# Channels dealt three to a partition, and two turns moved from TensorE to VectorE

## The chip, the cores and the metric

The kernel runs on one core of one Trainium2 chip. The metric is the device time of a launch in microseconds (us); the times here are the median of three runs. A profiled execution is a further run of its own: its trace has a span, from the first to the last instruction, and the run a time of its own beside it.

On a core there are five engines with queues of their own: TensorE (PE in the profile, with its weight loads as PEld), VectorE (DVE), ScalarE (ACT), GpSimd (POOL) and SyncE (SP, which in this kernel only issues transfers). Sixteen DMA engines move data between DRAM and the on-chip memory SBUF. TensorE writes into PSUM, which is divided into banks.

## The reference

x has the shape (8, 56, 56, 384), float32: 8 images of 56 by 56 positions with 384 channels. Two layers follow one another, each of them `x = x + f(gn(x))`.

```python
def _gn(v, G=32, eps=1e-5):
    g = v.reshape(B_, H_, W_, G, C_ // G)          # 32 groups of 12 channels
    m = jnp.mean(g, axis=(1, 2, 4), keepdims=True)
    s = jnp.var(g, axis=(1, 2, 4), keepdims=True)
    return ((g - m) / jnp.sqrt(s + eps)).reshape(v.shape)

# layer 0: 12 heads of 32 channels, 9 by 9 weights at each position
v = einsum('bhwc,oc->bhwo', x, Wv)
a = einsum('bhwc,oc->bhwo', x, Wa)                 # 972 logits a position
attn = softmax(a * 32 ** -0.5)                     # over the 9 inputs q
out = einsum('bnhpq,bnqhd->bnphd', attn, v_unf)    # v_unf: the 3 by 3 neighbours of v
canvas[:, i:i + h, j:j + w] += out[:, :, :, p]     # each of 9 outputs added at its place
y = canvas[:, 1:-1, 1:-1];  return einsum('bhwc,oc->bhwo', y, Wo)

# layer 1: 6 heads of 64 channels, 9 weights at each position
a = softmax(x @ W_attn + b_attn);  v = x @ W_v + b_v
y = einsum('bpKhd,bphK->bphd', patches_of_v, a);  return y @ W_proj + b_proj
```

## The kernel before

**Tiling.** The 8 images are taken as 4 pairs (`NPAIR`). A pair has 56 columns, and a column of a pair is 112 rows (`R`: two images of 56). A projection contracts over channels, so most of the work is done with the channels on the partitions: a tile is [128 partitions, 3 chunks (`NCH`), columns, 112 rows], and chunk i holds the channels 128i to 128i+127. In DRAM the channels are innermost. x is therefore turned once on its way in and the result once on its way out.

**Layer 0** goes one column a step, 56 steps a pair and three more at the end. In a step:

- `attend` (L604) makes three products of 288 logits (`wa_t`) and one of 384 (`wv_t`), each from three chunks, into PSUM `bank`s. VectorE takes the maximum and the difference out of the bank, ScalarE the exponential, and ScalarE copies v out. Between the products the hook `between` puts in other work.
- A step later the weights are normalised (VectorE, then GpSimd); then terms of neighbouring columns are added (`presum`) and a matmul into `pw` adds those of neighbouring rows (`fold`). SP stores the results in a table in DRAM (`ztab<-wts`), GpSimd stores v in another (`vtab<-v`).
- Of eight columns (`SB`) one has no tile of its own: its 112 rows ride in the 16 unused rows of each of the seven others; `share_out` (L647) brings their weights together (`last<-at`, `at<-last` on SP; `at<-at` on GpSimd).
- Every 7 columns make a patch. SP loads its two halves of v (`vp<-vtab`) and of the folded weights (`z<-ztab`), TensorE contracts them (`pc<-z,vp`), ScalarE copies to `yT`, and six `project_out` (L833) multiply by `wo_t` into `po`, PSUM tag "o", one buffer. VectorE adds the residual (`x1t`) and takes its statistics, and SP stores `x1t` to DRAM as layer 1's input. `plan` (L791) gives each of these pieces the step at which it is due; two or three pieces run in a step.

While pair p is worked on, x of pair p+1 is turned, in 14 blocks of 4 columns (`XB`), three steps a block. `stats_load` (L432) is one transfer on SP's queue of 112 partitions by 1536 floats (`xr<-in_x`). `stats_chunk` (L443) runs once a step: four TensorE transposes into `pt` (PSUM tag "t"), a ScalarE copy to `xt`, and two `bn_stats` on VectorE. After three chunks `keep_block` stores the block in DRAM (`xT<-xt` on SP), from where it is loaded again as `xin` and `xres`. x of pair 0 is turned at the start, before the first step, in the same way through the large banks.

After the last block, `norm_params` (L268) puts together the statistics: six `bn_aggr`, then an average over each group for the mean and another for the variance (L274 `over_groups`), into `pgmean` and `pgvar`. A group of 12 channels can lie across two chunks, so an average is seven matmuls with the matrices `gmat` (built at L153 to L169 from a selector, through three matmuls at the start). `normed` (L575) applies scale and bias on ScalarE, one instruction for each chunk and image, two blocks ahead of the products.

**Layer 1** (L998) works in 32 patches of 7 columns: `attend` makes one product of 438 columns (54 logits and v) into one of two banks, GpSimd stores both (`at<-lgt`, `vtab<-v`; L1075 and L331), then `weigh`, `share`, `move` and `fetch` lead to contractions (`pc`) and six `project_out` (L1180), PSUM tags "o" and "f". `turn` (L1190) brings a column back: three TensorE transposes, a ScalarE copy to `ot`, and after each half patch (4 and 3 columns) one GpSimd transfer of 112 partitions by 1536 or 1152 floats. Columns 3 to 6 of a patch wait in the list `turning` and alternate with the next patch's contractions, which run two (`NC`) at a time.

**What sets the order.** Each engine runs its instructions in the order of the program (`keep_in_program_order`, `InOrder`). Pieces in `jobs` run once their step is due, as many as the step calls for. Transfers go through one queue for each issuing engine; SP's carries all of layer 0's loads and stores but those of v and `at<-at`.

Of the kernel before, what the change touches and what calls it, by code (L numbers as in the profile page):

```python
# [15 lines left out]
def two_outlook_layers(  # L16
# [81 lines left out]

    xf = x.rearrange("b y x c -> (b y) x c")
# [52 lines left out]
    near = [range(max(0, i - 1), min(NCH, i + 2)) for i in range(NCH)]  # L152
    gmat = [const.tile([P, len(near[i]), P], F32, name=f"gmat_{i}") for i in range(NCH)]  # L153
    with tc.tile_pool(name="ps_setup", bufs=2, space=PS) as ps_setup:
        gsel = yT_flat[:G, :C]
        gpsimd.memset(gsel, 1.0)
        gpsimd.affine_select(
            out=gsel, in_=gsel, compare_op=ALU.is_ge, fill=0.0,
            base=0, pattern=[[1, C]], channel_multiplier=-GC,
        )  # L160
        gpsimd.affine_select(
            out=gsel, in_=gsel, compare_op=ALU.is_ge, fill=0.0,
            base=GC - 1, pattern=[[-1, C]], channel_multiplier=GC,
        )
        for i in range(NCH):
            pg = ps_setup.tile([P, C], F32, tag="pg", name=f"pg_{i}")
            matmul(pg, gsel[:, i * P : (i + 1) * P], gsel, start=True, stop=True)
            lo, hi = near[i][0] * P, (near[i][-1] + 1) * P
            nc.vector.tensor_scalar_mul(gmat[i].rearrange("p j c -> p (j c)"), pg[:, lo:hi], 1.0 / GC)  # L169
# [93 lines left out]
    def weight(pool, src, n, name, queue=nc.sync):  # L263
        t = pool.tile([P, NCH, n], F32, name=name)
        queue.dma_start(t, src.rearrange("(i p) n -> p i n", p=P))
        return t

    def norm_params(st, name, params, key):  # L268

        mv = stat.tile([P, NCH, IMG, 2], F32, tag="mv", name=f"mv_{name}")  # L270

        def over_groups(src, what):
            pg = ps.tile([P, NCH, IMG], F32, tag="t", name=f"p{what}_{name}")
            for j in range(NCH):  # L274
                for i in near[j]:
                    matmul(
                        pg[:, j, :], gmat[i][:, j - near[i][0], :], src[:, i, :],
                        start=(i == near[j][0]), stop=(i == near[j][-1]),
                    )
            g = stat.tile([P, NCH, IMG], F32, tag=what, name=f"{what}_{name}")  # L280
            vector.tensor_copy(g, pg)
            return g

        for i in range(NCH):
            for b in range(IMG):
                vector.bn_aggr(mv[:, i, b, :], st[:, i, b, :, :])
        yield
        mean = over_groups(mv[:, :, :, 0], "gmean")

        part = stat.tile([P, NCH, IMG], F32, tag="part", name=f"part_{name}")  # L290
        vector.tensor_sub(part, mv[:, :, :, 0], mean)
        vector.tensor_mul(part, part, part)
        vector.tensor_add(part, part, mv[:, :, :, 1])
        yield
        var = over_groups(part, "gvar")
        std = stat.tile([P, NCH, IMG], F32, tag="std", name=f"std_{name}")
        scalar.activation(std, var, AF.Sqrt, bias=eps_t)
        scale = const.tile([P, NCH, IMG], F32, name=f"scale_{name}")
        vector.reciprocal(scale, std)
        bias = const.tile([P, NCH, IMG], F32, name=f"bias_{name}")  # L300
# [93 lines left out]
    scalar.dma_start(bo_t, bo1.rearrange("(i p) -> p i", p=P))  # L394
# [25 lines left out]
    def layer0(late, pools):  # L420
# [11 lines left out]
        def stats_load(pair, blk, queue, xr):  # L432
            queue.dma_start(xr, xf[pair * R : (pair + 1) * R, blk * XB : (blk + 1) * XB, :])
            xrs[pair, blk] = xr

        def xr_tile(pair, blk):
            return io.tile([P, XB, C], F32, tag="xr", name=f"xr_{pair}_{blk}")[:R]
# [5 lines left out]
        def stats_chunk(pair, blk, i):  # L443

            if blk == 0 and i == 0:
                stats[pair] = stat.tile([P, NCH, IMG, NBLK, 6], F32, tag="st0", name=f"st0_{pair}")
# [3 lines left out]
            if pair == 0:  # L450
                pt = bank(P, 0, XB * R).rearrange("p (m r) -> p m r", m=XB)
            else:
                pt = ps.tile([P, XB, R], F32, tag="t", name=f"pt_{pair}_{blk}_{i}")
            for j in range(XB):
                transpose(pt[:, j, :], xr[:, j, i * P : (i + 1) * P], ident[:R, :R])
            scalar.copy(xt[:, i], pt)
            yield
            for b in range(IMG):
                vector.bn_stats(stats[pair][:, i, b, blk, :], xt[:, i, :, b * H : (b + 1) * H])
# [54 lines left out]
        for blk in range(NBLK):  # L514
# [5 lines left out]
            if blk == 1:  # L520
                wv_t = weight(fixed, wv0, C, "wv0_t", sync)
# [31 lines left out]
        scalar.dma_start(wn, wa0.rearrange("(i p) n -> p i n", p=P))  # L553
# [21 lines left out]
        def normed(g, chunks, whole=True, shared=True, both=False):  # L575
# [3 lines left out]
            for i in chunks:  # L579
                for b in range(IMG):  # L580
                    rows = slice(b * H, (b + 1) * H)

                    def put(dst, src):
                        if both and b:
                            vector.tensor_scalar(
                                dst, src, scale[:, i, b : b + 1], bias[:, i, b : b + 1],
# [291 lines left out]
        def upkeep(step):  # L878
# [18 lines left out]
            if j < NCH and g < NPAIR * NBLK:  # L897
                normed(g, (j,))
# [406 lines left out]
```

## Time and profile before

| | before |
|---|---|
| runs: median (lowest to highest) | 3314.91 us (3310.96 to 3317.94) |
| the profiled execution | 3315.84 us |
| its span in the trace | 3314.0 us, mean granted TensorE clock 0.978 |
| a pair in layer 0, from the trace | 522.7 us: 56 steps of 9.33 us |
| a patch in layer 1, from the trace | 34.3 us |
| DMA moved in the span | 850.99 MB, mean 257 GB/s |

How to read it: the busy share of an engine is its working time over the span. The page gives it as a total and, in 40 slices of the span, in tenths. A line of a group names the source line, the engine, the operation, output and inputs with their shapes, how often it ran, then its total busy time in us, the mean of one in ns, and the idle time just before such instructions with what ended it. Layer 0 takes about the first 2200 us and layer 1 the rest.

### The profile page before, as it was taken

The page shows a single profiled execution, that of the slowest core. Times are in us where ns is not written, and L with a number is a line of the kernel's source. Part 1 is how long each engine was busy: PE and PEld are TensorE (multiplying, and loading weights), DVE is VectorE, ACT ScalarE, POOL GpSimd, SP SyncE. Part 2 cuts the span into 40 slices and gives each one's busy share as a digit, 9 for nine tenths or more (in the row PEclk, how much of TensorE's full clock was granted, in tenths as well). Part 3 has the DMA queues.
Part 4 walks back from the last instruction along what each step waited for, and adds up shares of the span by engine and source line. Part 5 has one row for each costly group of instructions (what it writes and reads, how often), then busy time and mean ns, then how long its engine had stood idle before and what let it go on. Part 6 is the DMA issues. An engine that isn't in the chain of part 4 may idle for free. (4 is left out here: it accounts for less than half of the span.)

```text
span 3314.0 us, 75237 instructions
## 1 busy us (share of the span) xinstructions
PE 3183.7 (96%) x28510; PEld 2186.6 (66%) x28510; DVE 1870.4 (56%) x4786; ACT 1366.3 (41%) x3749; POOL 1565.1 (47%) x2375
## 2 busy tenths in 40 slices
PE   7899999999999999999999999899999999999998
PEld 5567767776777667677666667556666666666665
DVE  5667776767777776777666677443333333333332
ACT  4444444444444444444343444234343443434432
POOL 2655555545555554455554555454343443434431
PEclk8899999999999999999999999899999999999999
DMA  9699988979897898899787888877778777787775
GB/s 294 201 308 295 303 274 270 292 258 304 300 315 235 279 308 266 290 294 300 229 257 259 288 253 294 285 240 212 220 215 233 212 216 226 220 222 214 223 215 155
DMA packets 554908, 850.99 MB, mean 257 GB/s; under 512 B 162174, under 2 KB 429954, under 8 KB 550450
## 3 DMA queue, kind: packets, MB, share of 16 engines
q1 hardware_dynamic: 448674, 672.76, 65.0%
q0 software_dynamic: 72016, 155.44, 14.7%
q10 hardware_dynamic: 33856, 17.98, 2.1%
q8 instruction: 225, 3.69, 0.5%
q14 instruction: 137, 1.12, 0.1%
HBM read 514.86 MB, written 322.17 MB: 253 GB/s over the span
## 5 line engine op out<-in xcount | busy, mean ns | idle before, releaser
L118 PE MATMUL bank<-wa_t,xn 128*128 128x288 f32 x3528 | 979.0, 415 | 3.5 <-ACT xn L133 2.1
L133 POOL TENSOR_TENSOR at<-at,den 128x972 f32<-128x972 f32 x196 | 440.5, 2247 | 859.3 <-DVE den L133 522.4
L118 PE MATMUL po<-yT,wo_t 128*128 128x448 f32 (+1 forms) x2304 | 821.0, 496 | 14.5 <-DVE x1t L133 12.0
L118 PEld LDWEIGHTS bank<-wa_t,xn 128*128 128x128 f32 x3528 | 652.9, 192 | 218.3 <-issue 22.2
L118 PEld LDWEIGHTS po<-yT,wo_t 128*128 128x128 f32 x2304 | 426.8, 191 | 296.0 <-issue 186.2
L133 ACT ACTIVATE at<-at 128x972 f32<-128x972 f32 (+1 forms) x228 | 215.8, 946 | 867.9 <-DVE at L133 860.5
L1075 POOL DMA_DIRECT2D at<-lgt x392 | 205.4, 527 | 616.3 <-DVE lgt L133 589.5
L118 PE MATMUL bank<-wc_t,xn 128*128 128x438 f32 x1176 | 477.8, 542 | 0.0
L133 DVE TENSOR_REDUCE mx<-bank 128x36 f32<-128x324 f32 x588 | 285.3, 485 | 340.6 <-PE bank L118 338.5
L118 PE MATMUL bank<-wv_t,xn 128*128 128x384 f32 x1176 | 417.3, 491 | 0.0
L118 PE MATMUL pc<-z,vp 121*32 121x49 f32 (+1 forms) x17664 | 374.7, 218 | 16.5 <-issue 10.3
L118 PEld LDWEIGHTS pc<-z,vp 121*32 121x32 f32 (+1 forms) x17664 | 337.8, 120 | 76.4 <-issue 51.0
L133 DVE TENSOR_TENSOR at<-bank,mx 128x324 f32<-128x324 f32 x588 | 291.4, 496 | 107.6 <-POOL pre L133 44.7
L118 PEld LDWEIGHTS bank<-wc_t,xn 128*128 128x128 f32 x1176 | 212.9, 190 | 169.4 <-issue 160.4
L118 PEld LDWEIGHTS bank<-wv_t,xn 128*128 128x128 f32 x1176 | 223.6, 192 | 134.8 <-issue 12.0
L133 DVE TENSOR_TENSOR lgt<-bank,ba_t 128x54 f32<-128x54 f32 x196 | 42.2, 215 | 455.8 <-PE bank L118 451.2
L133 POOL DMA_DIRECT2D vtab<-v x476 | 290.4, 614 | 14.4 <-issue 8.1
L133 ACT COPY yT<-pc 128x294 f32<-128x294 f32 (+2 forms) x512 | 195.7, 407 | 187.3 <-PE pc L118 186.4
L133 POOL TENSOR_TENSOR pre<-at,at 112x108 f32<-112x108 f32 (+1 forms) x440 | 224.4, 527 | 68.7 <-DMA at<-at 48.8
L133 DVE SCALAR_TENSOR_TENSOR x1t<-po,bo_t,x1t 128x448 f32<-128x448 f32 (+1 forms) x156 | 97.6, 626 | 249.5 <-PE po L118 249.5
L133 ACT COPY ot<-pt 112x384 f32<-112x384 f32 x128 | 61.2, 478 | 411.3 <-PE pt L121 411.0
L331 POOL DMA_DIRECT2D vtab<-v x392 | 211.4, 543 | 11.6 <-DMA vtab<-v 6.4
(118 smaller groups left out, 3279.0 us busy)
## 6 DMA issues: line engine op xcount, KB each, us to landing
z<-ztab SPq DMA_DIRECT2D x64, 2352.0 KB
vp<-vtab SPq DMA_DIRECT2D x64, 1536.0 KB
vp<-vtab SPq DMA_DIRECT2D x64, 945.0 KB
xres<-xT SPq DMA_DIRECT2D x32, 1176.0 KB
ztab<-wts SPq DMA_DIRECT2D x336, 110.2 KB
vtab<-v POOLq DMA_DIRECT2D x108, 336.0 KB, 6.2
xin<-xT SPq DMA_DIRECT2D x52, 672.0 KB
xr<-in_x SPq DMA_DIRECT2D x50, 672.0 KB
```

The lines of the kernel that those rows point to most:

```text
L118: tc.keep_in_program_order(nc.tensor.matmul(*args, **kwargs))
L133: return lambda *args, **kwargs: tc.keep_in_program_order(op(*args, **kwargs))
L331: queue.dma_start(bass.AP(table.tensor, table.offset + first, [*([line * step, count] for step, count in rows_of or ((1, rows),)), *([[(R ...
L1075: nc.gpsimd.dma_start(at_of(g_of)[row : row + n, m_of].rearrange("r k h -> r (k h)"), lg[lo : lo + n])
```

## The change

**The channels are dealt out.** Partition p of chunk i holds channel 3p+i, where it held 128i+p. The weights are loaded in that order (`rows_of_channels`), with three rows together on a partition. The output columns of the two output projections have to be in the same order, so that layer 0's result has its channels as x has; `wo0` and `wo1` are loaded as before into spare tiles and their columns sorted by three copies each (`sort_columns`: VectorE at steps 5 to 7, GpSimd at the start of layer 1).

**x of pairs 1 to 3 is turned by VectorE.** Four SP transfers bring a block, one for each set of 32 partitions, in the order of `by_quadrant`: 4 columns by 112 rows, each a piece of 96 floats. On a partition then lie 14 pieces of 96 floats, and one `vector.transpose` a chunk turns every third float of them, in 32 by 32 pieces, into `xt`. PSUM and ScalarE are not used for it. Pair 0's x is still turned by TensorE, with a stride of three.

**The results are turned by VectorE** straight after the residual is added, three turns a half patch, into `ot`, and leave in four GpSimd transfers a half. `turn` and `turning` go away, and contractions stand alone in their jobs. `project_out` alternates between the PSUM tags "o" and "t" in both layers, and layer 1's `attend` uses all three banks.

**One matmul an average.** 12 channels now lie on 4 whole partitions, so statistics are put together over the chunks by `bn_aggr` and one 128 by 128 matrix (1/4 where two partitions share a group) averages a group. Scale and bias are [128, 2], and `normed` does all chunks of an image in one instruction.

```diff
+    def by_quadrant(ap, r0, col, n, b):
+        first = r0 * W * C + col * C + b * QC
+        return bass.AP(ap.tensor, ap.offset + first, [[C, n], [W * C, R], [1, QC]])
...
+    gmat = const.tile([P, G, NPG], F32, name="gmat")
+    gpsimd.memset(gmat, 1.0 / NPG)
...
+    def rows_of_channels(t, src, queue):
+        queue.dma_start(t, src.rearrange("(p i) n -> p i n", i=NCH))
+
+    def sort_columns(t, by, i, engine):
+        engine(
+            t[:, i].rearrange("k (j p) -> k j p", j=NCH), by[:, i].rearrange("k (p j) -> k j p", j=NCH)
+        )
...
-            pg = ps.tile([P, NCH, IMG], F32, tag="t", name=f"p{what}_{name}")
-            for j in range(NCH):
-                for i in near[j]:
-                    matmul(
-                        pg[:, j, :], gmat[i][:, j - near[i][0], :], src[:, i, :],
-                        start=(i == near[j][0]), stop=(i == near[j][-1]),
-                    )
+            pg = ps.tile([P, IMG], F32, tag="t", name=f"p{what}_{name}")
+            matmul(pg, gmat, src, start=True, stop=True)
...
         def stats_load(pair, blk, queue, xr):
-            queue.dma_start(xr, xf[pair * R : (pair + 1) * R, blk * XB : (blk + 1) * XB, :])
             xrs[pair, blk] = xr
+            if not pair:
+                queue.dma_start(xr, xf[:R, blk * XB : (blk + 1) * XB, :])
+                return
+            for b in range(NQ):
+                queue.dma_start(
+                    xr[b * Q : (b + 1) * Q].rearrange("p a c -> p (a c)"),
+                    by_quadrant(x, pair * R, blk * XB, XB, b),
+                )
...
             else:
-                pt = ps.tile([P, XB, R], F32, tag="t", name=f"pt_{pair}_{blk}_{i}")
-            for j in range(XB):
-                transpose(pt[:, j, :], xr[:, j, i * P : (i + 1) * P], ident[:R, :R])
-            scalar.copy(xt[:, i], pt)
+                vector.transpose(
+                    xt[:, i].rearrange("p m r -> p (m r)").rearrange("p (k a) -> p a k", a=NB),
+                    xr[:, :, i::NCH],
+                )
...
+                    by = z_flat[0][:, : NCH * C].rearrange("p (i n) -> p i n", i=NCH)
+                    sync.dma_start(by, wo0.rearrange("(i p) n -> p i n", p=P))
+                if 5 <= c < 5 + NCH:
+                    by = z_flat[0][:, : NCH * C].rearrange("p (i n) -> p i n", i=NCH)
+                    sort_columns(wo_t, by, c - 5, vector.tensor_copy)
...
-            pa = bank(P, 0, NC1, 2)
+            pa = bank(P, 0, NC1)
...
-                po = ps.tile([P, 4 * R], F32, tag="of"[(half * NCH + j) % 2], name=f"po1_{g}_{half}_{j}")
+                po = ps.tile([P, 4 * R], F32, tag="ot"[(half + j) % 2], name=f"po1_{g}_{half}_{j}")
...
+                if j == 0:
+                    fetch.ot = io.tile([P, NB, QC], F32, tag="ot", name=f"ot_{g}_{half}")
+                vector.transpose(
+                    fetch.ot[:, :, j::NCH],
+                    x1t[:, j, hi - XB : hi].rearrange("p m r -> p (m r)").rearrange("p (k a) -> p a k", a=NB),
+                )
+                if j == NCH - 1:
+                    n = (hi - lo) * Q // XB
+                    for b in range(NQ):
+                        nc.gpsimd.dma_start(
+                            by_quadrant(out, pair * R, px * PX + lo, hi - lo, b),
+                            fetch.ot[(b + 1) * Q - n : (b + 1) * Q].rearrange("p a c -> p (a c)"),
+                        )
...
```

## The prediction

> **What bounds the kernel now.** I read the page first, then stretches of 100 us, then TensorE's timeline, then the groups with their shapes kept apart, and last the transfers.
>
> ```profile
> span 3314.0 us, 75237 instructions
> ...
> PE 3183.7 (96%) x28510; PEld 2186.6 (66%) x28510; DVE 1870.4 (56%) x4786; ACT 1366.3 (41%) x3749; POOL 1565.1 (47%) x2375
> ...
> DMA  9699988979897898899787888877778777787775
> ```
>
> TensorE is busy 96% of the span, so its work is what counts while nothing else fills up. Next is the DMA row: eights and nines for the first two thirds (layer 0), sevens after that (layer 1). Two stretches tell the layers apart (PE, PEld, DVE, ACT, POOL busy us, clock, DMA share, GB/s):
>
> ```profile
> 1400.00:1500.00 100.00, 99.69 (x866) 71.59 (x865) 75.72 (x203) 43.30 (x114) 48.73 (x65) 1.00 0.93 305
> 2700.00:2800.00 100.00, 100.00 (x795) 63.33 (x794) 31.88 (x69) 42.19 (x123) 41.80 (x80) 1.00 0.77 218
> ```
>
> Layer 1 is TensorE without a gap, everything else half free. In layer 0 TensorE is nearly as full, but the DMA engines stand at 0.93 and VectorE at 76%. What a turned block costs TensorE is read from the starts in its timeline: from a group's start to the next start.
>
> ```profile
> 806.81 1.62 PE L118 MATMUL bank<-wa_t,xn 128*128 128x288 f32 x6
> 808.26 0.55 PE L121 MATMUL pt<-ident,xr 112*128 112x112 f32 x4
> 808.65 2.43 PE L118 MATMUL po<-yT,wo_t 128*128 128x448 f32 x6
> ...
> 2702.04 0.49 PE L121 MATMUL pt<-ident,x1t 128*112 128x128 f32 x3
> 2702.36 1.86 PE L118 MATMUL po<-yT,wo_t 128*128 128x336 f32 x6
> ```
>
> Four transposes of x take 808.65 - 808.26 = 0.39 us and three of a result 0.32, less than their busy times of 0.55 and 0.49, because matmuls overlap. The groups that price the rest (busy us, mean ns of one, idle before):
>
> ```profile
> L121 PE MATMUL pt<-ident,xr 112*128 112x112 f32 x504 | 69.7, 260 | 7.4 <-DMA xr<-in_x 7.4
> L118 PE MATMUL pgvar<-part,gmat 128*128 128x2 f32 x112 | 20.3, 311 | 5.4 <-DVE part L133 4.5 <-DVE part L293 0.9
> L133 DVE TENSOR_TENSOR d<-at 128x432 f32<-128x432 f32 x196 | 118.7, 606 | 19.7 <-ACT at L133 19.5
> L133 DVE TENSOR_REDUCE mx<-at 112x42 f32<-112x378 f32 x32 | 26.7, 836 | 0.0
> L1048 POOL DMA_DIRECT2D wc_t<-in_wv x1 | 0.8, 767 | 0.0
> ```
>
> And the transfers that share SP's queue with the x loads:
>
> ```profile
> q1 hardware_dynamic: 448674, 672.76, 65.0%
> ...
> z<-ztab SPq DMA_DIRECT2D x64, 2352.0 KB
> ...
> xr<-in_x SPq DMA_DIRECT2D x50, 672.0 KB
> ...
> last<-at SPq DMA_DIRECT2D x140, 60.8 KB
> ```
>
> **What the change takes off TensorE.** Summed from start to next start over the whole timeline: the 504 transposes of x 54.4 us, the 672 of the results 86.9, the 224 matmuls of the group averages 36.4. The averages become 16 matmuls, at 0.31 us each 5 us: 31 saved. The three selector matmuls at the start (4.2) save nothing: the x loads are waited for behind them. At two pair changes pgmean waits 3.9 us for a copied x tile; that wait goes: 8. Under TensorE alone: 54.4 + 86.9 + 31 + 8 = 180 us.
>
> **What it adds to VectorE.** 126 turns of x (42 blocks by 3) and 192 of results, 448 elements a partition each. No row shows such a turn. The plain row (432 elements) says 606 ns, the strided reduction 836 for 378, so 0.63 to 1.0 us; the other side of the plain row is nothing gained, since each still reads and writes 448 elements. I take 0.7, nearest the plain row: 88 us in layer 0, 134 in layer 1. In layer 1 that is 4.2 us in a patch of 34.3 where VectorE works 10.9 (two patches from 2700): hidden under TensorE. In layer 0 VectorE goes from some 72 to 80 us in 100: hidden, with perhaps 10 us of late bank releases; at 1.0 us some 25. Without that cover the 88 would be paid. Queued behind a turn that waits for its x are the maxima that free TensorE's banks; before, TensorE itself waited there (7.4 us), so I count no difference. The three copies that sort wo (about 0.5 us each) and the merged bn_aggr (fewer) are within this. [...]
>
> ScalarE loses the copies of turned tiles and two of three normalising instructions; it is at 41% and gives nothing back. The first product now waits for all three chunks, about 1 us once. The second PSUM buffer for po takes the 11 us for which TensorE waits on x1t in layer 0; I leave that against VectorE's 10. GpSimd issues 256 output transfers of 448 or 336 pieces instead of 64 of 112: 0.77 us (384 pieces) against 0.54, so 256 x 0.8 - 35 = 170 us in layer 1's 1100, where it is 41% busy; behind them wait the stores of logits and v, by at most 4 x 0.8 = 3.2 us, and these are needed several columns (4.9 us each) later. The two wo sorts wait for their loads: 3 us at the start; strided weight reads 2; tail 4 x 0.8 instead of 0.5: 3. Together +8.
>
> **What it does to the DMA engines.** This decides. A block of x was one transfer, 112 rows of 6144 bytes; now it is four, one for each 32 partitions, each 448 pieces of 384 bytes, and the DRAM side's outermost size is 4 columns. The trace has a transfer of that build: last<-at writes 2 by 8 rows of 3888 bytes, and its 16 packets of 152 ns start two at a time every 148 ns, so two engines carry it, eight packets after one another. Counting for each of SP's 1519 transfers the largest number up to 16 that divides the outermost size of both sides gives 21,708, and q1's packet records hold exactly 21,708 packets of 4 bytes, one for each engine that reports. Outermost 4 and 32 thus mean 4 engines. Whether the four transfers share the same four: at<-last (40 rows, ten engines) goes out as two transfers half a microsecond apart; their packets stand at ten at once for 7.7 us and above ten for 1.3, so transfers use the same first engines. So 4 x 448 / 4 = 448 packets fall on each of four engines in every block, where 7 fell on each of sixteen.
>
> Price of a 384-byte packet: quick ones of 336 bytes take 21 ns, of 504 bytes 27, so 23; the means (22 and 32) give 25. Load of these engines before, from the packets of one pair (850 to 1372.7 us, 522.7 us): at quick-quartile durations 0.75 over sixteen engines, 0.71 without x; the two engines that carry last<-at (560 packets x 152 / 2 = 43 us a pair) have 411 us in 522.7, that is 0.79. A block is three steps, 28.0 us. After: 0.79 x 28.0 + 448 x 23 ns = 22.0 + 10.3 = 32.3 us in 28.0: these engines are overfull and set the pace, TensorE's 26.7 no longer does. With mean durations 24.8 + 11.2 = 36.0. I take 33.0, near the quick end, because the other twelve engines get idler. The z and vp loads, spread over sixteen, end with their slowest share; the ztab stores issued behind x wait up to 10.3 us, and with them SP's eight transfers in flight; then TensorE waits for z. SP's own issuing (126 more at some 0.6 us) is not the limit.
>
> [...]
>
> **The sum.** 42 blocks x (33.0 - 28.0) = +210, which swallows the 54.4 of x transposes. Span 3314.0 - 86.9 (results) - 31 - 8 + 210 + 8 = 3406. The profiled run took 3315.84, 1.8 more than its span, and lies 0.9 above the median 3314.91: 3407, say 3410.
>
> **Rivals.** (1) Not slower: TensorE stays the bound, because the four transfers of a load spread over all engines (112 packets x 23 ns = 2.6 us each) or packets overlap better than I think. For it: layer 0 already runs stretches at 0.93 without a gap in TensorE. Against: the ten-at-once plateau. 3314 - 180 + 8 + 0 to 10 = about 3145. It decides when a block needs under 26.7 us; the break-even with before is 42 x (b - 28.0) = 86.9 + 31 + 8 - 8 = 118, b = 30.8 us.
> (2) Between: the engines bind mildly, b = 30 us: 3407 - 42 x 3 = 3281.
> (3) The output transfers, too, sit on a fixed four engines: 3136 packets a patch / 4 x 23 ns = 18.0 us on top of some 18.4 (0.584 of 34.3 at quick durations, less the old output's 1.6) = 36.4 us a patch in place of 34.3: layer 1 loses 67 instead of gaining 87, total 3561. For it the same rule; against, that queue is GpSimd's own, and its two-transfer stores of 8 rows show no plateau that I can read.
> (4) A turn costs far more: above 2.2 us VectorE is full in layer 0 (376 busy + 42 turns in 495 us of a pair, 95%). No row is near.
>
> **Chances.** Forecast (b 31 to 37, 3320 to 3550) 0.58, (1) 0.17, (2) 0.08, (3) 0.12, (4) 0.05. Range: quick end b = 30 less a little, 3240, to case (3) with a slower block, 3620; (1) is left out. About 0.2% (7 us) is what a measurement can tell. Faster: (1) and half of (2), 0.21; same 0.02; slower 0.77.
>
> **What would show it.** Right: TensorE busy share in layer 0 down to about 80 to 88%, idle before pc and pw, DMA share in the first three pairs lower, not higher, with SP waiting on transfers; three steps near 33 us in pairs one to three but still 28 in the fourth; a patch in layer 1 near 31.6 us; pgmean and pgvar eight each. Wrong: three steps at 26 to 27 us, which is rival (1); a patch above 34 us, rival (3); StreamTranspose above 1 us, rival (4).

## The result and the profile after

The changed kernel takes 3601.75 us (median of four runs, 3574.94 to 3619.56) against 3316.43 before in the same comparison: a ratio of 1.0855, interval 1.0785 to 1.0925. It is slower, as forecast, but by 285 us and not by 95. The profiled execution took 3600.22 us, its span is 3598.5. From its page:

```profile
span 3598.5 us, 71850 instructions
...
PE 3160.0 (88%) x27136; PEld 2087.5 (58%) x27136; DVE 2143.7 (60%) x5068; ACT 1020.5 (28%) x2736; POOL 1816.3 (50%) x2570
...
DMA  8578787787779778778878887989889889888875
...
q1 hardware_dynamic: 518978, 672.76, 60.3%
...
DMA 23%; PE 7%; POOL 4%; issue 2%; DVE 1%; ACT 0%; POOLq 0%; SPq 0%; DVEq 0%; ACTq 0%
```

TensorE's share falls from 96% to 88%, though it has less to do. The DMA row, which stood at eights and nines in layer 0 and at sevens in layer 1, is now the other way round: sevens and eights first, eights and nines in layer 1. The last line above is the chain that ended last (the work that, followed back from the end, each step had waited for). Before, that line read:

```profile
PE 33%; issue 2%; DVE 1%; DMA 0%; ACT 0%; POOL 0%; ACTq 0%; POOLq 0%; SPq 0%; DVEq 0%
```

TensorE held 33% of the span there and now holds 7%; DMA holds 23%, and the page lists 13 of these for `out<-ot`. The same two stretches as before, in the same columns (PE, PEld, DVE, ACT, POOL busy us, clock, DMA share, GB/s):

```profile
1400.00:1500.00 100.00, 89.46 (x694) 61.18 (x692) 75.24 (x191) 28.88 (x79) 43.39 (x56) 0.97 0.80 261
2700.00:2800.00 100.00, 93.33 (x722) 55.55 (x721) 43.81 (x78) 24.41 (x72) 58.81 (x84) 0.98 0.91 209
```

In layer 0 the share of the DMA engines has gone down, from 0.93 to 0.80, and TensorE with it. In layer 1 it has gone up, from 0.77 to 0.91, while the bytes went down, from 218 to 209 GB/s: the same data cost the engines more time. The groups (busy us, mean ns of one, idle before and what ended it):

```profile
L1211 POOL DMA_DIRECT2D out<-ot x256 | 283.5, 1178 | 186.0 <-DMA out<-ot 90.6 <-DVE ot L142 50.5 <-DMA at<-lgt 11.7
...
L142 DVE TENSOR_TENSOR lgt<-bank,ba_t 128x54 f32<-128x54 f32 x196 | 41.0, 209 | 530.8 <-DMA at<-lgt 393.9 <-PE bank L127 130.9 <-PE pc L127 3.3
...
L142 DVE STREAM_TRANSPOSE ot<-x1t 128x448 f32<-128x448 f32 x156 | 150.9, 967 | 5.8 <-DMA out<-ot 0.4
L142 DVE STREAM_TRANSPOSE xt<-xr 128x448 f32<-128x448 f32 x126 | 121.1, 961 | 39.3 <-DMA xr<-in_x 38.4 <-DMA ztab<-wts 0.8
```

The logit row of the kernel before, beside it:

```profile
L133 DVE TENSOR_TENSOR lgt<-bank,ba_t 128x54 f32<-128x54 f32 x196 | 42.2, 215 | 455.8 <-PE bank L118 451.2 <-DMA vtab<-v 3.0 <-DMA at<-lgt 1.5
```

VectorE had waited 451.2 us for TensorE before it took the logits out of the bank; now most of its 530.8 us are `DMA at<-lgt`, that is, it waits for a free logit tile whose store has not landed. A turn takes 0.96 us.

Stages are read from the starts of TensorE's groups: a pair from its first product of v to that of the next pair, layer 0 up to the first product of layer 1, a patch from one `pw` to the next (mean).

| | forecast | before | after |
|---|---|---|---|
| second pair, third pair, us | | 522.4, 523.4 | 570.7, 571.1 |
| layer 0 ends at | +176 | 2152.4 | 2301.5 (+149) |
| a patch in layer 1 | 31.6 | 34.1 | 38.0 |
| first product of layer 1 to TensorE's last | -87 | 1150.5 | 1276.4 (+126) |
| TensorE's last to the end of the span | +3 | 11.1 | 20.5 (+9) |

The forecast of +176 is its +210 less the 31 and 8, with 5 of the small items. So layer 0 as a whole lost somewhat less than was forecast; layer 1 should have gained and lost instead.

Where layer 0 loses is seen in SP's queue (start, duration of the issues, count):

```profile
1023.46 5.47 SPq L142 DMA_DIRECT2D ztab<-wts  x4
1028.99 10.56 SPq L142 DMA_DIRECT2D xr<-in_x  x4
1039.65 2.12 SPq L142 DMA_DIRECT2D last<-at  x1
1041.87 2.93 SPq L142 DMA_DIRECT2D ztab<-wts  x4
```

Four x loads hold SP for 10.56 us here. Over all blocks of the three pairs a load takes SP 2.57 us on average, where the one load of a block took 0.62, and from 700 to 1700 us SP spends 763 us on issuing transfers instead of 389; what stands behind, such as `ztab<-wts`, starts later. How that reaches TensorE is read from the waits of that stretch (total, times, longest; the first two rows are TensorE's):

```profile
PE bank L127 <- DVE at L142: 44.8, 24, 4.7
PE pc L127 <- DMA z<-ztab: 8.6, 2, 4.5
ACT wts L142 <- DMA ztab<-wts: 178.6, 36, 15.9
DVE wts L142 <- DMA ztab<-wts: 49.8, 16, 7.0
DVE at L142 <- DMA last<-at: 38.5, 9, 10.5
DVE xt L142 <- DMA xr<-in_x: 28.0, 8, 5.1
```

ScalarE and VectorE wait for transfers of SP's queue, VectorE then frees the banks late, and TensorE waits for a bank. In the kernel before, TensorE has no wait of the first kind in this stretch. Where layer 1 loses is seen in its timeline:

```profile
2762.86 0.50 POOL L1089 DMA_DIRECT2D at<-lgt  x1 [2.55 <-DMA out<-ot]
2764.62 0.55 POOL L1089 DMA_DIRECT2D at<-lgt  x1 [1.25 <-DMA out<-ot]
2766.69 1.08 POOL L328 DMA_DIRECT2D vtab<-v  x2 [1.53 <-DMA out<-ot]
2767.41 0.21 DVE L142 TENSOR_TENSOR lgt<-bank,ba_t 128x54 f32<-128x54 f32 x1 [8.34 <-DMA at<-lgt]
...
2768.00 0.68 DVE L142 SCALAR_TENSOR_TENSOR x1t<-po,bo_t,x1t 128x448 f32<-128x448 f32 x1
...
2768.73 5.35 PE L127 MATMUL po<-yT,wo_t 128*128 128x336 f32 x12 [3.25 <-DVE x1t L142]
```

GpSimd cannot issue the logit stores, since an output transfer eight places ahead has not landed (the trace has its 1631 transfers on eight semaphores in turn, 203 or 204 on each, and an issue waits on the semaphore that it uses, so the ninth waits for the first); VectorE waits 8.34 us for a logit tile; the addition that frees `po` stands behind it on VectorE, and TensorE waits 3.25 us for that.

### The profile page after: what moved, and what is told of

It is laid out like the page before. It is cut to its first block, busy times and chain, and to the rows that moved or that the text cites. A ratio compares the mean times of both kernels' runs of the same rounds, so it can differ in the third digit from the quotient of the medians.

```text
span 3598.5 us, 71850 instructions
## 1 busy us (share of the span) xinstructions
PE 3160.0 (88%) x27136; PEld 2087.5 (58%) x27136; DVE 2143.7 (60%) x5068; ACT 1020.5 (28%) x2736; POOL 1816.3 (50%) x2570
## 3 DMA queue, kind: packets, MB, share of 16 engines
q1 hardware_dynamic: 518978, 672.76, 60.3%
## 5 line engine op out<-in xcount | busy, mean ns | idle before, releaser
L127 PE MATMUL bank<-wa_t,xn 128*128 128x288 f32 x3528 | 1005.6, 424 | 57.8 <-DVE at L142 53.0
L127 PE MATMUL po<-yT,wo_t 128*128 128x448 f32 (+1 forms) x2304 | 859.2, 517 | 130.0 <-DVE x1t L142 83.5
L127 PEld LDWEIGHTS bank<-wa_t,xn 128*128 128x128 f32 x3528 | 664.7, 197 | 295.0 <-DVE at L142 86.2
L127 PEld LDWEIGHTS po<-yT,wo_t 128*128 128x128 f32 x2304 | 451.4, 199 | 455.1 <-issue 201.5
L127 PEld LDWEIGHTS pc<-z,vp 121*32 121x32 f32 (+1 forms) x17664 | 354.7, 125 | 180.1 <-issue 110.2
L127 PE MATMUL bank<-wv_t,xn 128*128 128x384 f32 x1176 | 428.0, 502 | 26.2 <-DVE at L142 26.2
L127 PE MATMUL pc<-z,vp 121*32 121x49 f32 (+1 forms) x17664 | 394.9, 224 | 55.3 <-ACT yT L142 25.7
L1211 POOL DMA_DIRECT2D out<-ot x256 | 283.5, 1178 | 186.0 <-DMA out<-ot 90.6
L142 DVE TENSOR_TENSOR lgt<-bank,ba_t 128x54 f32<-128x54 f32 x196 | 41.0, 209 | 530.8 <-DMA at<-lgt 393.9
L1089 POOL DMA_DIRECT2D at<-lgt x392 | 217.9, 581 | 187.6 <-DMA out<-ot 101.9
L142 ACT ACTIVATE wts<-pre,inside 112x48 f32<-112x48 f32 (+4 forms) x672 | 179.8, 356 | 315.4 <-DMA ztab<-wts 269.1
```

What stands on the lines that cost most here:

```text
L127: tc.keep_in_program_order(nc.tensor.matmul(*args, **kwargs))
L142: return lambda *args, **kwargs: tc.keep_in_program_order(op(*args, **kwargs))
L1089: nc.gpsimd.dma_start(at_of(g_of)[row : row + n, m_of].rearrange("r k h -> r (k h)"), lg[lo : lo + n])
L1211: nc.gpsimd.dma_start(by_quadrant(out, pair * R, px * PX + lo, hi - lo, b), fetch.ot[(b + 1) * Q - n : (b + 1) * Q].rearrange("p a c -> p ...
```

## The experiments

Each is the changed kernel with one edit, unless said otherwise. A single run has one time. "Layer 1" in the expectations counts from its first product to the end of the span.

### Output transfers on SP's queue

```diff
-                        nc.gpsimd.dma_start(
+                        nc.sync.dma_start(
                             by_quadrant(out, pair * R, px * PX + lo, hi - lo, b),
```

> Kernel after, with the output transfers (same pieces, same four a half patch) issued by SP instead of GpSimd. After has layer 1 at 1297.0 us (from its first product, at 2301.5, to the end at 3598.5), before 1161.6. Theory A (GpSimd's queue: an output transfer lands after 10 to 12 us, at most eight of its transfers are under way, so its issues wait, the stores of logits wait behind them, then VectorE for a free logit buffer, then TensorE): layer 1 falls to TensorE's bound, some 1075 us (1161.6 less 87), span 3377. Theory B (384-byte pieces on a fixed four engines, the forecast's rival 3): 36.4 us a patch, layer 1 some 1229, span 3530. If layer 1 stays within 20 us of 1297 both are wrong. Layer 0 unchanged within 10 us.

Measured: 3683.82 us, 40.3 us a patch, layer 1 1375 us, layer 0 at 2306.8. Both forecasts miss, A's by far, and layer 1 is worse. But A's chain of waits is gone, as the logit row shows:

```profile
L142 DVE TENSOR_TENSOR lgt<-bank,ba_t 128x54 f32<-128x54 f32 x196 | 42.1, 215 | 297.3 <-PE bank L127 295.0 <-issue 2.3
```

VectorE no longer waits for a logit store (393.9 us after the change), so the output transfers on GpSimd's queue were what delayed these stores. The price has moved to SP, whose timeline reads:

```profile
2722.37 16.45 SPq L1211 DMA_DIRECT2D out<-ot  x4
2738.93 2.27 SPq L142 DMA_DIRECT2D x1t<-x  x1
2741.31 14.36 SPq L1211 DMA_DIRECT2D out<-ot  x4
2755.89 2.11 SPq L142 DMA_DIRECT2D vp<-vtab  x1
```

Four output transfers hold SP for 14 to 16 us. Over the whole layer one takes 3.60 us on average, and from 2450 to 3200 us SP spends 672 of 750 us on issuing: SP sets the patch. This queue's packets (q1) rise from 518978 to 620226, by 101248; the pieces are 128 x 448 + 128 x 336 = 100352; the other 896 are 128 x 4 + 128 x 3, as if each transfer of a half of four columns had four packets of 4 bytes and each of three columns three. No record names an engine. That one packet of 4 bytes stands for one engine is my reading; it rests on the kernel before, where `last<-at` (two of them by the forecast's count) had its packets at two at once and `at<-last` (ten) at ten, and it fits the changed kernel, where the 384-byte packets of the x loads (four) stand at four or five at once for 271 of the 467 us in which there are any, and above five for 43. Engines are counted in this way in what follows. Here that gives four and three engines, and for both 112 pieces an engine. A packet of 384 bytes takes 25.4 ns on average in this stage, so 112 of them 2.8 us; the issue takes longer than that, and the rest is not explained.

### The same, a transfer for each column

```diff
-                    n = (hi - lo) * Q // XB
-                    for b in range(NQ):
-                        nc.gpsimd.dma_start(
-                            by_quadrant(out, pair * R, px * PX + lo, hi - lo, b),
...
+                    for m in range(lo, hi):
+                        for b in range(NQ):
+                            at = (b + 1) * Q - (hi - m) * R // NB
+                            nc.sync.dma_start(
+                                by_quadrant(out, pair * R, px * PX + m, 1, b),
+                                fetch.ot[at : at + R // NB].rearrange("p a c -> p (a c)"),
+                            )
```

> Kernel after, with the output on SP and one transfer for each column and quarter (28 a patch, each 112 pieces, outermost sizes 112 and 8, so eight engines by the rule). A alone: as the run with four a half, about 1075 us for layer 1, span 3377. B: 18.4 us of other load and 3136 x 22 ns / 8 = 8.6 us make 27 a patch, below TensorE's 31: 1075 too, clearly under the run with four engines. If instead the number of transfers decides (28 and ten loads a patch, eight under way, 8 us each), 38 us a patch and layer 1 at 1220 or more.

Measured: 3935.89 us, 48.1 us a patch, layer 1 1621 us. q1 has 626498 - 518978 - 100352 = 7168 = 896 transfers x 8 packets more than the pieces, which counts as eight engines, but it is slower than with four, so few engines alone do not set this price. By the expectation's third case the number of transfers decides; that case gave 38 us a patch, ten too few. SP spends only 363 of 750 us on issuing (2450 to 3200 us); what fills the rest was not followed up.

### One contiguous x load a block

```diff
-            for b in range(NQ):
-                queue.dma_start(
-                    xr[b * Q : (b + 1) * Q].rearrange("p a c -> p (a c)"),
-                    by_quadrant(x, pair * R, blk * XB, XB, b),
-                )
+            queue.dma_start(
+                xr.rearrange("p a c -> p (a c)"),
+                bass.AP(
+                    x.tensor, x.offset + pair * R * W * C + blk * NB * QC,
+                    [[R * W * C // P, P], [1, NB * QC]],
+                ),
+            )
```

> Kernel after, with x of pairs two to four loaded by one transfer a block of 128 partitions by 1344 contiguous floats (sixteen engines by the rule, the same bytes, the same turns by VectorE); x arrives in other places than the turn expects, so the values are not the reference's. Theory C (the four engines of the x loads set the block): a pair goes from 570.8 us to TensorE's bound, 522.5 less 18 for the transposes and some 8 for the averages, 495 to 505; layer 0 at 2301.5 less 200 to 225. Theory D (VectorE's turn, 0.97 us and not 0.7, releases the banks late): a pair stays above 550. Layer 1 unchanged within 20 us.

Measured: 3443.54 us; pairs of 523.3 and 520.9 us, layer 0 at 2140.7, a patch 38.0. The loads make up nearly all that a pair lost (570.7 to 523.3, against 522.4 before). The rest of C, 495 to 505 us, does not come: a second limit lies at about 522.

### An x load for each column

```diff
-                queue.dma_start(
-                    xr[b * Q : (b + 1) * Q].rearrange("p a c -> p (a c)"),
-                    by_quadrant(x, pair * R, blk * XB, XB, b),
-                )
+                for m in range(XB):
+                    at = b * Q + m * R // NB
+                    queue.dma_start(
+                        xr[at : at + R // NB].rearrange("p a c -> p (a c)"),
+                        by_quadrant(x, pair * R, blk * XB + m, 1, b),
+                    )
```

> Kernel after, with the x loads one for each column and quarter (16 a block, outermost sizes 112 and 8, eight engines by the rule). C: 224 pieces of 23 ns on each of eight engines, 5.2 us on top of 22.0 a block, about TensorE's own 27: a pair 500 to 520 us, layer 0 at 2301.5 less 150 to 210. D: a pair above 550. If SP's number of transfers decides (12 more a block), a pair above 570.8.

Measured: 3686.38 us; pairs of 597.8 and 601.6 us. C misses, and the last case, a pair above 570.8, comes true. The packets of 4 bytes on q1 come to eight a load (26412 - 21708 = 4704 more, which is 672 x 8 - 168 x 4). A load takes SP 0.74 us on average instead of 2.57, but there are sixteen, and a block's loads hold SP for 14.5 us from the first to the last, where the four held it for 10.5.

### The same pieces and transfers in another order, for the output

Still four transfers a half and pieces of 384 bytes; only the order in which the DRAM side counts rows and columns is turned round.

```diff
+    def by_rows(ap, r0, col, n, b):
+        first = r0 * W * C + col * C + b * QC
+        return bass.AP(ap.tensor, ap.offset + first, [[W * C, R], [C, n], [1, QC]])
...
-                            by_quadrant(out, pair * R, px * PX + lo, hi - lo, b),
+                            by_rows(out, pair * R, px * PX + lo, hi - lo, b),
```

> Kernel after, with the DRAM side of each output transfer in the order row, column, 96 channels instead of column, row, 96 channels: the same number of transfers on GpSimd's queue, the same 384-byte pieces, but outermost sizes 112 and 32 (or 24), so sixteen (or eight) engines by the rule instead of four (or one). The elements land in other places, so the values are not the reference's. After has 37.98 us a patch from one pw to the next, before 34.12. Theory E (few engines): a patch of 31 to 33 us. Theory G (the pieces, whatever engines carry them): 37 to 38. Layer 0 unchanged within 10 us.

Measured: 3414.40 us, 32.8 us a patch, layer 0 at 2297.7. (On SP's queue above, a half of three columns had three packets of 4 bytes and not one, as the expectation has it for engines; on GpSimd's queue no count shows it.) This one swap takes the whole loss of layer 1 away and more. Its stretch and its groups:

```profile
2700.00:2800.00 100.00, 97.32 (x736) 58.40 (x736) 48.65 (x87) 24.22 (x70) 57.38 (x96) 0.98 0.86 229
```

```profile
L1215 POOL DMA_DIRECT2D out<-ot x256 | 213.5, 840 | 269.2 <-DVE ot L146 253.0 <-issue 8.1 <-DVE mx L146 7.9
...
L146 DVE TENSOR_TENSOR lgt<-bank,ba_t 128x54 f32<-128x54 f32 x196 | 42.1, 215 | 295.2 <-PE bank L131 290.1 <-issue 3.6 <-DMA at<-lgt 1.5
```

TensorE is at 97 us in 100 again; VectorE's wait for `at<-lgt` has gone from 393.9 us to 1.5, and what it waits for is TensorE, as before the change. The time from issue to landing (the last number, a median in us) falls with it. In the changed kernel it was

```profile
out<-ot POOLq DMA_DIRECT2D x128, 168.0 KB, 9.8
out<-ot POOLq DMA_DIRECT2D x128, 126.0 KB, 11.9
```

and here it is

```profile
out<-ot POOLq DMA_DIRECT2D x128, 168.0 KB, 7.0
out<-ot POOLq DMA_DIRECT2D x128, 126.0 KB, 3.7
```

Even the issue on GpSimd is cheaper, 0.84 us in place of 1.18.

### Large pieces for the output

```diff
+                        first = (pair * R * W + px * PX * R + lo * R) * C + b * n * NB * QC
                         nc.gpsimd.dma_start(
-                            by_quadrant(out, pair * R, px * PX + lo, hi - lo, b),
+                            bass.AP(out.tensor, out.offset + first, [[NB * QC, n], [1, NB * QC]]),
```

> Kernel after, with each output transfer written as 32 (or 24) pieces of 5376 contiguous bytes: the same number of transfers on GpSimd's queue, the same bytes and turns, sixteen (or eight) engines; the elements land in other places, so the values are not the reference's. E and G both: 31 to 33 us a patch. Theory T (the number of transfers, 32 a patch with at most eight under way): 36 to 38 us.

Measured: 3427.48 us, 32.8 us a patch. Pieces fourteen times as large bring nothing that the order had not brought already, and 32 transfers a patch are no obstacle: G and T fall. E is what is left of the theories tried; no run shows the engines on this queue.

### More buffers between VectorE and GpSimd's stores

```diff
-            lg = work.tile([P, NA1], F32, tag="lgt", name=f"lgt_{col}", bufs=4)
+            lg = work.tile([P, NA1], F32, tag="lgt", name=f"lgt_{col}", bufs=12)
...
-            v = work.tile([P, C], F32, tag="v", name=f"v_1_{col}", bufs=5)
+            v = work.tile([P, C], F32, tag="v", name=f"v_1_{col}", bufs=9)
```

> Kernel after, with twelve buffers for logits instead of four and nine for v instead of five, so that VectorE need not wait for a late store of GpSimd's for nine columns. If the late stores only come in bursts (theory L, latency): VectorE's waits for at<-lgt, some 12.7 us a patch, go, and a patch falls to 32 to 35 us. If GpSimd's queue is full on average (E, G or T), the same backlog fills the new buffers too: 37 to 38 us.

Measured: 3602.38 us, 38.2 us a patch. Theory L falls. The queue is not late now and then; it takes longer than a patch on average, and more buffers only hold a longer backlog.

### The same pieces and loads in another order, for x

The edit is `by_rows` for `by_quadrant` in the x loads.

> Kernel after, with the DRAM side of each x load in the order row, column, 96 channels: still four loads a block of 448 pieces of 384 bytes, but outermost sizes 112 and 32, sixteen engines instead of four. x arrives in other places than the turn expects, so the values are not the reference's. If the four engines made the loads dear: a pair of 520 to 525 us as with one contiguous load (521 to 523). If the pieces or the number of loads did: 555 to 571.

Measured: 3436.48 us; pairs of 521.8 and 522.4 us, layer 0 at 2144.0. From its page and the stretch at 1400 us:

```profile
span 3434.8 us, 71850 instructions
...
DMA  9799898899888989988778788898888888888875
...
q1 hardware_dynamic: 520994, 672.77, 64.0%
```

```profile
1400.00:1500.00 100.00, 96.87 (x776) 66.82 (x779) 83.10 (x213) 31.68 (x83) 48.00 (x64) 1.00 0.92 293
```

q1 has 520994 packets, 2016 more than after: 168 loads with 12 more packets of 4 bytes each, sixteen for four. A load now takes SP 0.89 us on average, and the DMA share is back at 0.92. Neither the small pieces nor the four loads cost the time, but the outermost size of 4.

### x turned by TensorE again

The load, the four transposes and ScalarE's copy of the kernel before are put back for pairs two to four (with `xr[:, j, i::NCH]`, as pair 0 has it); the rest is as in the changed kernel.

> Kernel after, with x of pairs two to four loaded and turned as before (one load a block, TensorE transposes, ScalarE copies), channels three to a partition, one matmul an average and the rest as in after. A pair took 522.4 us before and 521.8 with VectorE's turn and loads on sixteen engines. Theory D2 (VectorE's turns give back what TensorE saves, since averages and banks wait for VectorE): without them a pair falls below both, to 510 to 517 us (522.4 less some 8 for the averages). If the averages save nothing or the clock is what binds: 520 to 524. Layer 1 as in after, 38 us a patch.

Measured: 3462.68 us; pairs of 524.5 and 528.5 us. Both bands missed. The largest wait of TensorE in 574 to 1618 us (total, times, longest) points to a reason, which the last run below tests:

```profile
PE po L127 <- ACT xt L142: 17.3, 12, 2.9
```

`po` alternates between the tags "o" and "t", and "t" is the buffer that the turned x passes through. The change frees "t" by moving the turn away; with the turn back, `project_out` waits for ScalarE's copies.

### Row by row, with every value in its place

For the output, tokens are counted row by row, four columns each. A turn then fills a chunk in two instructions, and each half writes four columns, the second half its column 3 again.

```diff
-                vector.transpose(
-                    fetch.ot[:, :, j::NCH],
-                    x1t[:, j, hi - XB : hi].rearrange("p m r -> p (m r)").rearrange("p (k a) -> p a k", a=NB),
-                )
+                for n, e, to in ((4, 0, 2 * R + 3), (3, 2, 4 - 2 * R)):
+                    vector.transpose(
+                        dims_of(fetch.ot[:, :, j::NCH], e * QC, [4 * QC, n], [QC, 2], [NCH, Q]),
+                        dims_of(x1t[:, j, hi - XB : hi], e * R, [1, n], [R, 2], [7, Q // 2], [to, 2]),
+                    )
...
-                            by_quadrant(out, pair * R, px * PX + lo, hi - lo, b),
-                            fetch.ot[(b + 1) * Q - n : (b + 1) * Q].rearrange("p a c -> p (a c)"),
+                            by_rows(out, pair * R, px * PX + hi - XB, XB, b),
+                            fetch.ot[b * Q : (b + 1) * Q].rearrange("p a c -> p (a c)"),
```

(`dims_of` sets the free dims of a tile.) First with x turned by TensorE, as in the run above:

> x loaded and turned as before, and the results turned by VectorE into the order row, column (two instructions a chunk instead of one), so that the output transfers have 112 rows outermost in DRAM and 32 partitions in SBUF, sixteen engines, 384-byte pieces; the second half patch writes its column 3 once more, with the same values. The result is the reference's. Engines theory: 32.8 to 33.5 us a patch, layer 0 as in the run with x turned by TensorE: 3250 to 3290 us in all. If the second write of column 3 makes GpSimd wait for the first half's landing (7 us): 34 to 36 us a patch, 3290 to 3360.

Measured: 3272.46 us (3267.64 to 3278.34), ratio 0.9866, interval 0.9849 to 0.9884; 32.9 us a patch, pairs of 525.2 and 527.9, all within the first band. The second write of column 3 is not felt. Then with x, too, loaded and turned in that order by VectorE:

> The change kept whole, with row, column order on both sides: x loads of four a block with 112 rows outermost (sixteen engines), turned by two VectorE instructions a chunk, and the outputs as in the run beside it. Engines theory: a pair of 520 to 526 us, 32.8 to 33.5 us a patch, 3265 to 3310 us in all, so faster than before by 0 to 1.5%. If the two instructions or their strides cost clearly more than one (over 1.3 us a chunk), a pair of 530 or more.

Measured: 3278.30 us (3274.61 to 3281.21), ratio 0.9886, interval 0.9869 to 0.9902; pairs of 526.2 and 526.1 (just above the band), 32.7 us a patch. The whole change, with two dims of each transfer exchanged, two turns a chunk and column 3 written twice, is 1.1% faster than the kernel before, a small gain, but its interval is clear of 1. Its groups show the price of the issue and of the two turns:

```profile
L1222 POOL DMA_DIRECT2D out<-ot x256 | 181.2, 714 | 283.8 <-DVE ot L156 241.2 <-issue 16.0 <-DVE mx L156 11.1
...
L156 DVE STREAM_TRANSPOSE xt<-xr 128x256 f32<-128x256 f32 x126 | 81.3, 646 | 0.1
...
L156 DVE STREAM_TRANSPOSE xt<-xr 128x192 f32<-128x192 f32 x126 | 68.0, 540 | 4.3
```

The two turns of a chunk take 0.65 + 0.54 = 1.19 us in place of 0.96. Last, x by TensorE with layer 0's `po` on tag "o" alone, as before the change:

```diff
-                po = ps.tile([P, 4 * R], F32, tag="ot"[(half + j) % 2], name=f"po_{nm}_{half}_{j}")
+                po = ps.tile([P, 4 * R], F32, tag="o", name=f"po_{nm}_{half}_{j}")
```

> As x_pe_out_row_ok, but layer 0's project_out uses PSUM tag o alone, as before, so that po no longer waits for the buffer that the turned x occupies (TensorE sat 17.3 us there in two pairs, waiting for ScalarE's copies to xt). If that sharing is what keeps a pair at 525 to 528 us: 514 to 519, and 3235 to 3255 us in all. If something else binds layer 0 near 522: 521 to 526, 3262 to 3275.

Measured: 3257.44 us (3249.81 to 3261.61), ratio 0.9814, interval 0.9787 to 0.9841; pairs of 518.3 and 518.5, layer 0 at 2133.4, 32.9 us a patch. The pairs are in the first band, the total 2 us above it: sharing the buffer was what kept the pairs at 525 to 528. From its page and stretches:

```profile
span 3254.1 us, 72950 instructions
...
PE 3104.4 (95%) x27640; PEld 2110.4 (65%) x27640; DVE 2075.5 (64%) x5134; ACT 1087.4 (33%) x2862; POOL 1711.0 (53%) x2570
...
DMA  9699988888997898988877887889888888888886
```

```profile
1400.00:1500.00 100.00, 99.69 (x961) 73.88 (x960) 76.22 (x206) 40.64 (x106) 52.97 (x71) 1.00 0.94 320
2700.00:2800.00 100.00, 98.81 (x744) 59.11 (x743) 51.87 (x107) 24.06 (x70) 56.91 (x100) 1.00 0.87 237
```

TensorE is at 99 us in 100 in both layers. This version keeps of the change the order of the channels, the single averages, the larger instructions of `normed` and the results' turn; it leaves the turn of x where it was.

## Why the prediction was right and wrong

**The x loads: the price near, the cause right, the path only in part.** Forecast were 33.0 us a block through four engines, 42 x 5.0 = 210. The three pairs with loads lost 62.7 + 48.3 + 47.7 = 158.7 us, or 31.8 us a block. That the outermost size of 4 is the cause is shown by the exchange of two dims. The path is another matter. The text had the four overfull engines set the pace and TensorE wait for z; TensorE's waits for z are 8.6 us in 1000, and its 44.8 us are for banks that VectorE frees late. And "SP's own issuing ... is not the limit" counted 0.6 us an issue, where 2.57 were measured. Four kernels show what SP has to do with it:

| x loads of a block | pieces for an engine in a load | one issue on SP, us | a block's loads hold SP, us | second and third pair, us |
|---|---|---|---|---|
| one contiguous, not counted (sixteen expected) | 8 (expected) | 0.63 | 0.6 | 523.3, 520.9 |
| four, 112 outermost, sixteen engines | 28 | 0.89 | 4.1 | 521.8, 522.4 |
| four, 4 outermost, four engines | 112 | 2.57 | 10.5 | 570.7, 571.1 |
| sixteen, one a column, eight engines | 14 | 0.74 | 14.5 | 597.8, 601.6 |

The pairs go with the time that the loads hold SP (0.6 and 4.1 us cost a pair nothing, 10.5 and 14.5 us do), and not with the number of engines alone: with eight engines, each of which gets half as much, a pair is longer than with four. So in place of engines that set the pace the runs show SP held, its stores and `last<-at` issued late, and ScalarE and VectorE waiting for them. Whether the load on single engines adds to that stays open.

**The results: here it failed.** The step is the sentence that hid the 256 output transfers: GpSimd "is 41% busy; behind them wait the stores of logits and v, by at most 4 x 0.8 = 3.2 us, and these are needed several columns (4.9 us each) later". The issue took 1.18 us and not 0.8, but that is the small part. The bound counted issuing time alone and left out that the ninth transfer waits until the first has landed, and that landing takes long: a median of 9.8 and 11.9 us for the two halves after, 7.0 and 3.7 in the kernel with exchanged dims. So the stores waited, VectorE's 8 us for a logit tile followed, and instead of -87 us layer 1 had +126. Two runs bear this chain out: with the outputs off GpSimd's queue, and with the dims exchanged on it, VectorE's waits for `at<-lgt` go from 393.9 us to under 2.

Rival (3) came nearest, at 0.12: it priced a patch at 36.4 us, and it was 38.0. That the numbers are close is luck. The price rested on 3136 packets of 384 bytes through a fixed four engines. On GpSimd's queue the record has nearly all of the pieces in 8960 packets of 4224 bytes, eleven pieces each, of 0.31 us on average, and they stand at one to twelve at once, with no step at four. The argument against the rival was that GpSimd's stores of eight rows showed no plateau either. That was too weak, as nothing on this queue counts engines: q0 has 3072 more packets of 4 bytes after the change, 16 for each of the 192 more transfers, though their outermost sizes are 4 and 3. Which engines carried them no record here names. What within the queue takes the 10 to 12 us stays open, too: with the dims exchanged, a kind of 44-byte packet also falls from 32000 to 3072, in the other runs with large outermost sizes it is gone, and no run separates the two.

**What should have been gained.** With the dims exchanged on both sides the gains are small. The results' turn: a patch goes from 34.1 to 32.8, 1.4 us of the forecast 2.7. The transposes are gone, but TensorE's other groups go from 31.4 to 32.3 us a patch, and some 0.5 us of waiting for `yT` comes in (summed from start to next start); why the groups take longer was not tried. The x turn: 54.4 us of TensorE work in three pairs and next to nothing gained, 521.8 us a pair with VectorE's turn and sixteen engines, against 522.4 before and 518.3 in the last version with TensorE's own turn (which also has other buffers for `po`). TensorE's largest waits in two pairs of the kernel with VectorE's turn and sixteen engines (574 to 1618 us; total, times, longest) read:

```profile
PE pw L131 <- ACT pre L146: 13.5, 4, 3.7
PE pgmean L131 <- DVE mv L146: 10.9, 2, 5.5
PE pgvar L131 <- DVE part L146: 9.3, 2, 4.7
PE bank L131 <- DVE at L146: 9.2, 12, 0.9
```

`pw` waited before, too (for GpSimd then); what is new is that the averages and the banks wait for VectorE, which is busy 822 of 1044 us (753 before). TensorE's idle time goes from 29 to 58 us, and its mean granted clock from 0.99 to 0.97. I had set VectorE's turn at 0.7 us, and it took 0.96; with 1.0 the forecast had put 25 us of late bank releases, which is nearer.

**The averages.** 31 us and the 8 of the wait on a copied tile were forecast. The rows count two records for a matmul of these: 32 records and 7.7 us are left after the change, and not 16 and 5, a small slip. The last version, which differs from before in layer 0 by the averages, the order of the channels and `normed`, gains 19.0 us there (2152.4 to 2133.4). The wait did not go: in two pairs of that version pgmean waits 6.2 us for a copied tile (7.7 before) and pgvar 7.0 us for VectorE (0.9 before), and with VectorE's turn both wait for VectorE, 10.9 and 9.3 us in the rows above. In the changed kernel this gain is covered by the loads.

**The sum.** The span was forecast at 3314 + 92 = 3406 and came to 3314 + 284.5. Of the difference of 192 us, 213 lie in the results' step and 6 in the tail, and layer 0 was overestimated by 27. That 27 is small partly by luck: the loads cost 51 us less than forecast, and the rest of layer 0 gained some 24 less. Of the other rivals, (1) falls because a load does not spread over all engines (q1 has 21708 packets of 4 bytes after as before, 168 x 4 of the loads' in place of 42 x 16), (2) because a block takes 31.8 us, and (4) because a turn takes 0.96 us and not 2.2.

## What to carry to other kernels

Read both sides of a transfer for their outermost size before anything else: 4 rather than 112 there turned a gain of some 1% into a loss of 8.6%, with pieces of the same size and the same number of transfers. When a queue gets more transfers, bound the wait behind them by the time to land and the number that may be under way, not by the issuing time. And when work moves off the busiest engine, ask which engine its neighbours now wait for; 54 us of TensorE work moved to VectorE brought next to nothing.

## What the runs showed of the hardware

- An issue of an x load on SP's queue took longer the more pieces there were to one of its packets of 4 bytes (an engine, as counted here): 0.62 us with 7 (before, 672 KB), 0.74 with 14 (an x load for each column, 42 KB), 0.89 with 28 (168 KB, sixteen such packets), 2.57 with 112 (after, the same 168 KB, four). As stores to DRAM on the same queue, issues with 112 took 3.60 us.
- A packet of 384 bytes on SP's queue took 23.6 ns on average on its way from DRAM on four engines by this count (31.8 on sixteen), and 25.4 ns on its way to DRAM on four or three.
- GpSimd's issue of an output transfer took 1.18 us on average with 4 or 3 outermost and 0.84 with 112, for the same pieces of 384 bytes.
- A VectorE turn of 448 float32 elements on 128 partitions took 0.96 us, and one of 256 elements 0.65: near the 1.0 us for 448 that the strided reduction gave, and far from the plain row's 0.63.
